# Four convolution layers on one core: another order for the last image of layer 1, the first signs' shift on another engine, narrower gate weights

## The chip, the cores and the metric

The kernel runs on one core of a Trainium2 chip. TensorE (PE in the profile; PEld is its weight load) multiplies matrices, VectorE (DVE), ScalarE (ACT) and GpSimd (POOL) do the rest, and SyncE (SP) issues most transfers. Each engine works through its own queue in order and waits on semaphores for the others. The metric is the device time of one execution in microseconds (us); less is better.

## The reference

Sixteen images of 256 channels and 28 x 28 pixels go through four layers. Layer 0 is a 3x3 convolution of signs, normalized over the batch, added to its input. Layer 1 is the one that the change touches; layer 2 is two more 3x3 convolutions of signs with batch norms, and layer 3 is attention over the 784 pixels of each image. Layer 1, cut to what matters:

```python
residual = prelu(x, a_alpha1)
y = conv3x3(sign(x + a_move), clip(a_w, -1, 1))
y = prelu(bn(y, a_bn1), a_alpha2)
y = se_gate(s * x + y * (1 - s)) * y          # first gate
y = bn(y * residual, a_bn2) + residual
u = conv1x1(sign(y + f_move), clip(f_w, -1, 1))
u = prelu(bn(u, f_bn1), f_alpha2)
u = se_gate(s2 * y + (1 - s2) * u) * u        # second gate
return bn(u, f_bn2) + y

def se_gate(mix):                             # per image
    h = relu(mix.mean(pixels) @ w1.T + b1)    # 256 -> 32
    return sigmoid(h @ w2.T + b2)             # 32 -> 256
```

Layer 2 begins with a batch norm over all images of layer 1's result, so it can't start before the last image's second gate is known.

## The kernel before

The 256 channels are two halves of 128 partitions (`k` for inputs, `mo` for outputs), and an image is a tile of 128 x 2 x 784. Layers run one after the other. In layers 0 to 2 each engine's order is the order in which the program's lines are called, under a manual schedule: no scheduler moves anything on TensorE, VectorE or ScalarE. `keep_busy(n)` puts n multiplications of a tile of zeros into TensorE's queue, whose result nobody reads.

**Layer 1's start.** `norm` (line 187) works out layer 0's scale `r` (`rsqrt`, line 137: a square root on ScalarE, the rest on VectorE) and two shifts, one for the sign (`zb1`) and one for the values (`bi0`). The shifts are made by three `nc.gpsimd.tensor_tensor` (lines 209 and 211). Its argument `then` issues `enter(0, 0)` on VectorE as soon as `r` is there; `sign1(0, 0)` on ScalarE needs both this and `zb1`. `transform` (line 696) then adds and subtracts neighbouring rows of the signs into `vs16`, `widen` copies that to `vs`, and TensorE convolves.

**The 3x3 convolution** (`conv`, line 724) makes two rows of output from four transformed inputs u = 0 to 3: for one `mo` and one `u`, 12 multiplications (6 of a high part of the weights with `vs16`, 6 of a low part with `vs`). `conv_pair` (743) collects u = 1 and 2 in the halves `i` = 0 and 1 of one PSUM tile, u = 0 and 3 in those of another; there are three such tiles of two banks (`psc`, line 427). `sum_pair_a` (754, ScalarE) and `sum_pair_b` (761, VectorE) turn the first pair into `uv`; `rows_out` (769, VectorE) adds each half of the second to it: one instruction for the even rows, one for the odd. `prelu_y` (789) finishes `y` and its sum.

**The gates.** Both gates of an iteration are asked together, since they are small: the first of image b-1, and the second of image b-2. `hidden_x` and `hidden_a` (792, 796) mix their sums into a tile `p` on VectorE, with one column for each gate, and multiply it with `w_1` (`hidden_sums`, 636), a tile of 128 columns in which 0 to 31 hold the first gate's weights, 32 to 63 the second's, and the rest zeros. `hidden_b` (802) makes the two relus on ScalarE; `gates` (809) multiplies with `w_2`, takes the sigmoid and a scale. `branch1_a`, `_b` and `_c` (822 to 835) apply the first gate and make the signs `z2` for `conv1x1` (839); `unit_u` and `unit_b` (854, 861) finish its result `u`; `branch2` (864) applies the second gate and sends the image to memory (`x2d`, GpSimd's queue, line 873). `squares2` (881) adds up squares for the next batch norm.

**The loop.** `iteration(b)` (888) interleaves three images: b in the convolution, b-1 at its first gate and conv1x1, b-2 at its second gate; `ahead` stands for the next image's entry, which the last iteration doesn't have. After the last (line 1017 on) comes a chain with one image left: both gates (image 15's first, image 14's second), image 15's branch 1 and conv1x1, `branch2` and `squares2` of image 14, then image 15's second gate, the moments of the batch norm (`moments1`) and the first signs of layer 2 (line 1110). `squares` and `products` write their full-size results, which nobody reads, into two buffers `rn` that they share.

Of the kernel before, what the change touches and what calls it, by code (L numbers as in the profile page):

```python
# [39 lines left out]
P = 128  # L40
# [43 lines left out]
def forward(ctx: ExitStack, tc: tile.TileContext, d: dict, out: bass.AP, careful: bool):  # L84
# [51 lines left out]

    def rsqrt(name, v, half=None):

        r, t = (const.tile(list(v.shape), F32, name=name + q) for q in ("_r", "_t"))
        A.activation(t, v, AF.Sqrt)  # L140
        V.reciprocal(r, t)
        tt(t, r, r, ALU.mult)
        if half is not None:
            tt(r, r, half, ALU.mult)
        else:
            V.tensor_scalar(r, r, -0.5, None, ALU.mult)
        tt(t, t, v, ALU.mult)
        V.scalar_tensor_tensor(r, t, -3.0, r, ALU.add, ALU.mult)
        return r
# [37 lines left out]
    def norm(name, moments, gamma, beta, sf=None, then=lambda r: None, shifts=()):  # L187


        half, e = vtile(name + "_half"), vtile(name + "_e")  # L190
        V.tensor_scalar(half, gamma, -0.5, None, ALU.mult)
        if sf is not None:

            tt(e, sf, sf, ALU.mult)
            V.tensor_scalar(e, e, 1e-30, 1.0 / EPS, ALU.max, ALU.mult)
            V.reciprocal(e, e)
        m, var = moments()
        v, c = vtile(name + "_v"), vtile(name + "_c")
        if sf is not None:
            tt(v, var, e, ALU.add)  # L200
        else:
            V.tensor_scalar(v, var, EPS, None, ALU.add)
        r = rsqrt(name, v, half)
        then(r)
        if not shifts:
            tt(c, m, r, ALU.mult)
            return r, tt(c, beta, c, ALU.subtract)
        cs = [vtile(f"{name}_c{i}") for i in range(len(shifts))]
        nc.gpsimd.tensor_tensor(c, m, r, ALU.mult)
        for o, b in zip(cs, shifts):  # L210
            nc.gpsimd.tensor_tensor(o, b, c, ALU.subtract)
        return r, *cs
# [214 lines left out]
    with tc.tile_pool(name="ps_conv", bufs=3, space=PSUM) as psc, \  # L427
# [13 lines left out]
        with tc.tile_pool(name="ph1", bufs=1) as ph:  # L441
# [106 lines left out]

            w_1, w_2, b_1 = (ph.tile(sh, F32, name=n) for sh, n in (([P, 2, P], "se1"), ([P, 256], "se2"), ([64, 1], "seb")))

# [84 lines left out]

            def hidden_sums(p):

                ps = pss.tile([P, 2], F32, tag="sm", name="hid")
                for k in range(2):
                    T.matmul(ps, lhsT=w_1[:, k, :], rhs=p[:, :, k], start=(k == 0), stop=(k == 1))  # L640
                return [ps[32 * g:32 * g + 32, g:g + 1] for g in range(2)]
# [100 lines left out]

            def conv_pair(b, mo, i, u):
                if i == 0:
                    pairs[b, mo, u > 0 and u < 3] = conv_ps()
                conv(b, mo, u, pairs[b, mo, u > 0 and u < 3][:, i, :HN])

# [20 lines left out]

            def rows_out(b, mo):
                ps, uv = pairs.pop((b, mo, False)), pairs.pop((b, mo))  # L770
                y = full("yu", f"y{b}_{mo}", 6)
                ys[b, mo] = y
                two = y.rearrange("p (a two b) -> p two a b", two=2, b=S)
                for i in range(2):
                    V.scalar_tensor_tensor(
# [15 lines left out]

            def hidden_x(t):
                p = small.tile([P, 2, 2], F32, tag="g0", name="g0")
                return tt(p, sums_of(t)[0], mix_x, ALU.mult)

            def hidden_a(t, p):

                r = small.tile([P, 2, 2], F32, tag="g1", name="g1")
                tt(r, sums_of(t)[1], mix_y, ALU.mult)
                return hidden_sums(tt(p, p, r, ALU.add))  # L800

            def hidden_b(t, sums):
                h = hidden[t % 3]
                for g, ps in enumerate(sums):
                    rows = slice(32 * g, 32 * g + 32)
                    A.activation(h[rows, g:g + 1], ps, AF.Relu, bias=b_1[rows])
                return h

            def gates(h, f=None):

                ps = pss.tile([P, 2, 2], F32, tag="sm", name="gate")
                g = small.tile([P, 2, 2], F32, tag="gate", name="gates")
                for k in range(2):
                    T.matmul(ps[:, k], lhsT=w_2[:, k * P:(k + 1) * P], rhs=h, start=True, stop=True)
                A.activation(g.rearrange("p i k -> p k i"), ps, AF.Sigmoid)
                if f is not None:
                    return tt(f, g[:, 1], s_bn[:, 3], ALU.mult)
                return tt(g, g, s_bn[:, 1::2], ALU.mult)

# [68 lines left out]
            def iteration(b):  # L888


                ahead, one, two = b + 1 < B, b >= 1, b >= 2
                if b + 2 < B:
# [9 lines left out]
                if two:  # L902
                    unit_u(b - 2, 1)
                if ahead:
                    enter(b + 1, 0, sc0)
                if one:
                    prelu_y(b - 1, 1)
                if ahead:
                    enter(b + 1, 1, sc0)
                    sign1(b + 1, 0)  # L910
                if two:
# [4 lines left out]
                h = hidden_a(b, hidden_x(b)) if one else None  # L916
                if ahead:
                    residual_a(b + 1, 0)
                    sign1(b + 1, 1)
                sum_pair_b(b, 0)  # L920
                if one:
                    h = hidden_b(b, h)
                if ahead:
                    residual_a(b + 1, 1)
                    residual_b(b + 1, 0)
                    transform(b + 1, 1)
                    residual_b(b + 1, 1)
                conv_pair(b, 0, 1, 3)
# [3 lines left out]
                else:  # L932
                    gate_bias()
                if ahead:
                    transform(b + 1, 2)
                if one:
                    for k in range(2):
                        branch1_a(b - 1, k, g[:, 0])
                if ahead:
                    widen(b + 1, 1)  # L940
                for i, u in enumerate((1, 2)):
# [10 lines left out]
                if one:  # L952
                    branch1_c(b - 1, 1)
                if ahead:
                    widen(b + 1, 2)
                if two:
# [6 lines left out]
                for s in aside[b + 1]:  # L963
                    s.load()
                if ahead:
                    for u in (0, 3):
                        transform(b + 1, u)
                        widen(b + 1, u)
                    for i, u in enumerate((0, 3)):
                        conv_pair(b, 1, i, u)  # L970
                    rows_out(b, 1)
                    for late in lates:
                        late()
                    if one:
                        conv1x1(b - 1)
                else:
                    conv1x1(b - 1)
                    for k in range(2):
                        unit_u(b - 1, k)
                        unit_b(b - 1, k)  # L980
                    for i, u in enumerate((0, 3)):
                        conv_pair(b, 1, i, u)
                    px = hidden_x(B)
                    rows_out(b, 1)
                    prelu_y(b, 1)
                    return px

# [5 lines left out]
            with tc.manual_schedule(engines={ET.PE, ET.DVE, ET.Activation}):  # L993
# [17 lines left out]
                for k in range(2):  # L1011
                    residual_b(0, k)
                for b in range(B):
                    px = iteration(b)


                b = B - 1
                keep_busy(14)
                g = gates(hidden_b(B, hidden_a(B, px)))
                keep_busy(14)  # L1020
# [14 lines left out]
                squares(x2[b][:, 0, :], shift[:, 0:1], sum_vv[:, 0:1])  # L1035
                for k in range(2):
# [5 lines left out]
                px = hidden_x(B + 1)  # L1042
                V.tensor_reduce(m1, sum_x2[:, :, 0:B - 1], AX.X, ALU.add)
# [737 lines left out]
```

## Time and profile before

| | us |
|---|---|
| median of 3 runs (lowest, highest) | 964.71 (964.29, 966.12) |
| profiled execution: its time | 964.49 |
| profiled execution: span, first to last instruction | 962.7 |
| busy in the span: TensorE | 942.6 (98%) |
| VectorE | 772.7 (80%) |
| ScalarE | 718.7 (75%) |
| GpSimd | 143.0 (15%) |
| layer 1: first to last convolution matmul | 115.6 to 448.9 |
| first matmul of layer 2 | 469.5 |

The span leaves out 1.8 us of the execution's time. A busy TensorE is not TensorE at its peak, and where `keep_busy` runs it is not even useful. In the rows below, "[2.97 <-POOL l_c]" means that the engine was idle for so long before the instruction, and what ended that. A group such as "x4" is a run of instructions of one line, given by its first start and the time to its last end. The granted clock is TensorE's, as a share of full speed.

### The profile page before, as it was taken

To read this page: it belongs to the slowest core of one execution; us is meant where nothing else is said; L and a number is where in the kernel's file an instruction comes from. 1 tells how busy PE (TensorE), PEld (TensorE's weight loads), DVE (VectorE), ACT (ScalarE), POOL (GpSimd) and SP (SyncE) were. 2 spreads that over 40 slices of the span, in tenths; PEclk is the share of its full clock that TensorE was granted. 3 is DMA by queue.
4 is the path that set the end of the run, shared out by engine and by line. 5 is a ranking of instruction groups with operands and counts; after the bars stand their busy time and mean duration, and the time that the engine had idled before them with its cause. 6 is when DMAs were issued, how large, how long until landed. Compare 5 with 4: busy or idle time off the path is not lost.

```text
span 962.7 us, 14797 instructions
## 1 busy us (share of the span) xinstructions
PE 942.6 (98%) x5615; PEld 582.4 (60%) x5615; DVE 772.7 (80%) x1416; ACT 718.7 (75%) x1198; POOL 143.0 (15%) x152
## 2 busy tenths in 40 slices
PE   8999999999999999999999999999999999999996
PEld 4555577788788788786555555555444444444442
DVE  4777798999988898976799988999656868677765
ACT  6887668888887888865888868888666666676652
POOL 3001100000000000000100000000145353434331
PEclk9999999999999999999999999999999999999998
DMA  9978512444433243000670000000143443435212
GB/s 352 343 267 292 192 34 84 139 143 153 146 104 101 101 134 117 34 35 34 253 316 1 1 1 2 1 1 1 16 79 75 90 113 81 121 73 130 67 67 105
DMA packets 26948, 105.82 MB, mean 110 GB/s; under 512 B 3490, under 2 KB 7268, under 8 KB 26868
## 3 DMA queue, kind: packets, MB, share of 16 engines
q1 hardware_dynamic: 20948, 73.44, 21.3%
q0 software_dynamic: 5632, 30.54, 11.6%
q8 instruction: 46, 0.75, 0.3%
q10 hardware_dynamic: 288, 0.80, 0.2%
q14 instruction: 34, 0.28, 0.1%
HBM read 72.67 MB, written 32.11 MB: 109 GB/s over the span
## 4 chain that ended last, share of the span: by engine, by line
PE 41%; DVE 7%; ACT 2%; issue 1%; DVEq 0%; ACTq 0%
PE cv L346 14%; PE sc L1356 8%; PE av L1377 8%; PE mi L1333 4%; DVE p L1144 2%; PE sm L1419 2%; PE mi L1437 2%; PE sm L1377 1%; DVE ab L360 1%; DVE l2c_fin L1146 1%; DVE l2b_fin L1146 1%; ACT fpads L1110 1%; ACT es L1360 0%; DVE r L1403 0%; DVE p L1320 0%
## 5 line engine op out<-in xcount | busy, mean ns | idle before, releaser
L346 PE MATMUL cv<-fpads,wpk 128*128 128x392 f16 (+1 forms) x1746 | 294.8, 331 | 2.4 <-DVE wpk L273 1.2
L730 PE MATMUL cv<-vs,w 128*128 128x392 bf16 (+1 forms) x1536 | 285.3, 354 | 2.3 <-DVE vs L134 2.3
L346 PEld LDWEIGHTS <-wpk 128*128 128x128 f16 x1746 | 169.1, 97 | 128.9 <-DVE wpk L273 2.9
L730 PEld LDWEIGHTS cv<-vs,w 128*128 128x128 f32 x768 | 142.1, 190 | 10.9
L1360 ACT ACTIVATE es<-sc 128x784 f32<-128x784 f32 x112 | 87.3, 822 | 41.4 <-PE sc L1356 41.4
L730 PEld LDWEIGHTS <-w 128*128 128x128 f16 x768 | 67.6, 101 | 57.0 <-issue 17.2
L1356 PE MATMUL sc<-q,keyswa 64*128 64x392 f32 x448 | 89.9, 513 | 0.9 <-ACT es L1360 0.9
L357 ACT ACTIVATE t<-cv,rounding 128x392 f32<-128x392 f32 (+2 forms) x82 | 52.0, 634 | 41.2 <-PE cv L346 41.2
L1144 DVE SCALAR_TENSOR_TENSOR p<-ab,vec 128x392 f32<-128x392 f32 x128 | 79.1, 618 | 2.3
L1377 PE MATMUL av<-es,v 128*64 128x392 f32 x448 | 80.7, 499 | 0.0
L1370 POOL TENSOR_TENSOR sum<-sum,es 128x784 f32<-128x784 f32 x32 | 67.2, 2099 | 3.1 <-ACT es L1360 0.6
L1356 PEld LDWEIGHTS sc<-q,keyswa 64*128 64x128 f32 x448 | 38.9, 186 | 44.0 <-issue 17.1
L873 POOL DMA_DIRECT2D x2d<-x x16 | 8.6, 537 | 339.7 <-DVE x L867 281.0
L1344 DVE COPY keyswa<-mi 64x392 f32<-64x392 f32 x31 | 16.3, 564 | 52.7 <-ACT q L1340 52.7
L1377 PEld LDWEIGHTS av<-es,v 128*64 128x64 f32 x448 | 29.4, 136 | 47.4 <-issue 47.0
L712 ACT CAST vs<-vs 128x840 fp32r<-128x840 bf16 x63 | 54.1, 882 | 2.9 <-DVE vs L134 2.9
L845 PE MATMUL cv<-z,fw 128*128 128x392 f32 x256 | 48.9, 342 | 1.0 <-ACT z L837 0.8
L360 DVE SCALAR_TENSOR_TENSOR ab<-ab,cv 128x392 f32<-128x392 f32 x64 | 35.4, 553 | 16.3 <-ACT ab L358 16.3
L845 PEld LDWEIGHTS cv<-z,fw 128*128 128x128 f32 x256 | 45.7, 188 | 2.3 <-ACT z L837 2.1
L1333 PE MATMUL mi<-p,wqk 128*128 128x392 f32 x124 | 45.1, 505 | 0.1
L439 PE MATMUL unused<-idle 128*128 128x512 bf16 x175 | 41.2, 393 | 3.0 <-POOL idle L475 3.0
L1368 POOL TENSOR_TENSOR sum<-es 128x784 f32<-128x784 f32 x16 | 30.0, 1877 | 91.0 <-ACT es L1360 91.0
(289 smaller groups left out, 1516.9 us busy)
## 6 DMA issues: line engine op xcount, KB each, us to landing
xs<-in_x_dram SPq DMA_DIRECT2D x30, 784.0 KB, 6.1
x2d<-x POOLq DMA_DIRECT2D x16, 784.0 KB, 3.6
out_dram<-p SPq DMA_DIRECT2D x15, 784.0 KB, 3.8
p<-x2d POOLq DMA_DIRECT2D x14, 784.0 KB, 6.8
p<-x2d SPq DMA_DIRECT2D x13, 784.0 KB, 15.4
n0d<-n POOLq DMA_DIRECT2D x16, 392.0 KB, 5.9
n<-n0d SPq DMA_DIRECT2D x16, 392.0 KB, 3.2
st<-in_w_dram SPq DMA_DIRECT2D x12, 384.0 KB, 6.4
```

Of the source, the lines that this page charges most:

```text
L346: T.matmul(pss[j][:, n // size if careful else h, :rows * S].rearrange("p (a b) -> p a b", b=S), lhsT=w[:, n, t, :], rhs=pads[:, blocks[j] ...
L357: A.activation(by_halves(t, blocks[j]), ps, AF.Identity, bias=rounding, scale=1.0 / PACK)
L360: V.scalar_tensor_tensor(a, b, -PACK, ps, ALU.mult, ALU.add)
L712: copy(v, w)
L730: T.matmul(ps.rearrange("p (a b) -> p a b", b=S), lhsT=w[:, k, c, u, mo * P:(mo + 1) * P], rhs=v[:, b % 2, u, k, :, c:c + S], start=((part ...
L845: T.matmul(ps[:, h, :HN], lhsT=w[:, k, mo * P:(mo + 1) * P], rhs=z2[b][:, k, h * HN:(h + 1) * HN], start=(k + i == 0), stop=(k + i == 2),)
L1144: V.scalar_tensor_tensor(p, y, alpha[:, mo:mo + 1], y, ALU.mult, ALU.max)
L1333: T.matmul(ps[:, h, :HN], lhsT=wqk[:, k, :], rhs=x[b][:, k, h * HN:(h + 1) * HN], start=(k == 0), stop=(k == 1))
L1356: T.matmul(ps[:, h, :HN], lhsT=chunk[rows], rhs=qs[b][rows], start=True, stop=True)
L1360: A.activation(e, ps[:, :, :HN], AF.Exp, scale=0.125)
L1370: (V if late else nc.gpsimd).tensor_tensor(sums[b, late], sums[b, late], e, ALU.add)
L1377: T.matmul(ps[64 * h:64 * h + 64, :HN], lhsT=w, rhs=e[:, h, :], start=start, stop=stop)
```

## The change

It has three parts.

1. **The last iteration gets a function of its own** (`last_iteration`), and `iteration` loses its `ahead` cases. In it the gates of the last regular kind come before the convolution of u = 0 instead of after it; conv1x1 of image 14 comes between the convolutions of u = 1 and 2 of the second half of the outputs; and image 14's second gate is asked alone, ahead of image 15's first. For that, `conv_pair` and `rows_out` can do their work in pieces, and the gates' functions take a slice (`ONE`, `TWO`) of their two columns. After the loop, only image 15's first gate is left to ask, `branch2` of image 14 is done, half of its squares are done on ScalarE and the other half becomes a product on VectorE, and the last gate asks for one column alone.
2. **The shifts of layer 0's norm** are made by four ScalarE activations of one column (two per shift) from `r` and the negated mean; that mean is negated on VectorE while it waits for the root.
3. **`w_1` has 64 columns** instead of 128, and so has the PSUM tile `hid` 64 partitions.

```diff
-    def rsqrt(name, v, half=None):
+    def rsqrt(name, v, half=None, beside=None):
...
         A.activation(t, v, AF.Sqrt)
+        if beside:
+            beside()
...
-        r = rsqrt(name, v, half)
+        r = rsqrt(name, v, half, (lambda: V.tensor_scalar(less, m, -1.0, None, ALU.mult)) if shifts else None)
...
-        nc.gpsimd.tensor_tensor(c, m, r, ALU.mult)
         for o, b in zip(cs, shifts):
-            nc.gpsimd.tensor_tensor(o, b, c, ALU.subtract)
+            for k in range(2):
+                A.activation(o[:, k:k + 1], r[:, k:k + 1], AF.Identity, bias=b[:, k:k + 1], scale=less[:, k:k + 1])
...
-            w_1, w_2, b_1 = (ph.tile(sh, F32, name=n) for sh, n in (([P, 2, P], "se1"), ([P, 256], "se2"), ([64, 1], "seb")))
+            w_1, w_2, b_1 = (ph.tile(sh, F32, name=n) for sh, n in (([P, 2, 64], "se1"), ([P, 256], "se2"), ([64, 1], "seb")))
...
-            def hidden_sums(p):
+            def hidden_sums(p, some=slice(0, 2)):
...
-                ps = pss.tile([P, 2], F32, tag="sm", name="hid")
+                ps = pss.tile([64, 2], F32, tag="sm", name="hid")
                 for k in range(2):
-                    T.matmul(ps, lhsT=w_1[:, k, :], rhs=p[:, :, k], start=(k == 0), stop=(k == 1))
+                    T.matmul(ps[:, some], lhsT=w_1[:, k, :], rhs=p[:, some, k], start=(k == 0), stop=(k == 1))
...
-            def conv_pair(b, mo, i, u):
-                if i == 0:
+            def conv_pair(b, mo, i, u, parts=range(2)):
+                if i == 0 and 0 in parts:
                     pairs[b, mo, u > 0 and u < 3] = conv_ps()
-                conv(b, mo, u, pairs[b, mo, u > 0 and u < 3][:, i, :HN])
+                conv(b, mo, u, pairs[b, mo, u > 0 and u < 3][:, i, :HN], parts)
...
-            def rows_out(b, mo):
+            def rows_out(b, mo, rows=range(2)):
...
-            def hidden_b(t, sums):
+            def hidden_b(t, sums, some=BOTH):
                 h = hidden[t % 3]
-                for g, ps in enumerate(sums):
+                for g, ps in list(enumerate(sums))[some]:
...
+            def last_iteration(b):
+
+                conv_pair(b, 0, 0, 1)
+                conv_pair(b, 0, 1, 2)
+                for k in range(2):
+                    unit_u(b - 2, k)
+                prelu_y(b - 1, 1)
+                for k in range(2):
+                    unit_b(b - 2, k)
+                sum_pair_a(b, 0)
+                h = hidden_b(b, hidden_a(b, hidden_x(b)))
+                conv_pair(b, 0, 0, 0)
+                sum_pair_b(b, 0)
+                g = gates(h)
+                for k in range(2):
+                    branch1_a(b - 1, k, g[:, 0])
+                conv_pair(b, 0, 1, 3)
+                branch2(b - 2, 0, g[:, 1])
+                for k in range(2):
+                    branch1_b(b - 1, k)
+                    branch1_c(b - 1, k)
+                conv_pair(b, 1, 0, 1)
+                rows_out(b, 0)
+                squares2(b - 2, 0)
+                branch2(b - 2, 1, g[:, 1])
+                conv1x1(b - 1)
+                sum_pair_a(b, 1)
+                prelu_y(b, 0)
+                conv_pair(b, 1, 1, 2)
+                for k in range(2):
+                    unit_u(b - 1, k)
+                    unit_b(b - 1, k)
+                squares2(b - 2, 1)
+                px = hidden_x(B, TWO)
+                conv_pair(b, 1, 0, 0, (0,))
+                h = hidden_a(B, px, TWO)
+                sum_pair_b(b, 1)
+                h = hidden_b(B, h, TWO)
+                conv_pair(b, 1, 0, 0, (1,))
+                rows_out(b, 1, (0,))
+                g = gates(h, some=TWO)
+                conv_pair(b, 1, 1, 3)
+                branch2(b - 1, 0, g[:, 1])
+                squares2(b - 1, 0)
+                px = hidden_x(B, ONE)
+                rows_out(b, 1, (1,))
+                prelu_y(b, 1)
+                keep_busy(10)
+                h = hidden_a(B, px, ONE)
+                branch2(b - 1, 1, g[:, 1])
+                return h
...
-                keep_busy(14)
-                g = gates(hidden_b(B, hidden_a(B, px)))
+                h = last_iteration(b)
+                g = gates(hidden_b(B, h, ONE), some=ONE)
...
-                for k in range(2):
-                    branch2(b - 1, k, g[:, 1])
-
-                products(x2[b][:, 1, :], shift[:, 1:2], x2[b][:, 1, :], sum_vv[:, 1:2])
+                for i, v in ((b, sum_vv[:, 1:2]), (b - 1, sum_sq[:, 1, b - 1:b])):
+                    products(x2[i][:, 1, :], shift[:, 1:2], x2[i][:, 1, :], v)
...
-                V.scalar_tensor_tensor(d1, shift, float(N), sv, ALU.mult, ALU.add)
+                tt(d1, sv, sum_x2[:, :, b - 1], ALU.add)
+                V.scalar_tensor_tensor(d1, shift, 2.0 * N, d1, ALU.mult, ALU.add)
...
-                h = hidden_a(B + 1, px)
                 for k in range(2):
-                    squares2(b - 1, k)
-                h = hidden_b(B + 1, h)
+                    squares(us[b, k], 0.0, sum_uu[:, k:k + 1], (B * N)**-0.5)
+                h = hidden_b(B + 1, hidden_a(B + 1, px, TWO), TWO)
...
-                squares(us[b, 0], 0.0, sum_uu[:, 0:1], (B * N)**-0.5)
...
-                g = gates(h, dqg[:, 2])
-                squares(us[b, 1], 0.0, sum_uu[:, 1:2], (B * N)**-0.5)
+                g = gates(h, dqg[:, 2], TWO)
```

More of the change, by code (lines that the diff above doesn't have):

```diff
@@ L197, in norm @@
         m, var = moments()
-        v, c = vtile(name + "_v"), vtile(name + "_c")
+        v, c, less = vtile(name + "_v"), vtile(name + "_c"), vtile(name + "_less") if shifts else None
         if sf is not None:
@@ L767, in sum_pair_b @@
                 pairs[b, mo] = uv
-            def rows_out(b, mo):
[L770 to L774, printed above, removed]
+            def rows_out(b, mo, rows=range(2)):
+                ps, uv = pairs[b, mo, False], pairs[b, mo]
+                if 0 in rows:
+                    ys[b, mo] = full("yu", f"y{b}_{mo}", 6)
+                two = ys[b, mo].rearrange("p (a two b) -> p two a b", two=2, b=S)
+                for i in rows:
                     V.scalar_tensor_tensor(
@@ L790, in prelu_y, with hidden_x, hidden_a @@
                 prelu(ys[b, mo], "a_alpha2", ra2, mo, sums_of(b + 1)[1][:, 0, mo:mo + 1])
-            def hidden_x(t):
+            BOTH, ONE, TWO = slice(0, 2), slice(0, 1), slice(1, 2)
+            def hidden_x(t, some=BOTH):
                 p = small.tile([P, 2, 2], F32, tag="g0", name="g0")
-                return tt(p, sums_of(t)[0], mix_x, ALU.mult)
-            def hidden_a(t, p):
+                tt(p[:, some], sums_of(t)[0][:, some], mix_x[:, some], ALU.mult)
+                return p
+            def hidden_a(t, p, some=BOTH):
                 r = small.tile([P, 2, 2], F32, tag="g1", name="g1")
-                tt(r, sums_of(t)[1], mix_y, ALU.mult)
-                return hidden_sums(tt(p, p, r, ALU.add))
-            def hidden_b(t, sums):
+                tt(r[:, some], sums_of(t)[1][:, some], mix_y[:, some], ALU.mult)
+                tt(p[:, some], p[:, some], r[:, some], ALU.add)
+                return hidden_sums(p, some)
+            def hidden_b(t, sums, some=BOTH):
                 h = hidden[t % 3]
-                for g, ps in enumerate(sums):
+                for g, ps in list(enumerate(sums))[some]:
                     rows = slice(32 * g, 32 * g + 32)
@@ L807, in hidden_b, with gates @@
                 return h
-            def gates(h, f=None):
+            def gates(h, f=None, some=BOTH):
                 ps = pss.tile([P, 2, 2], F32, tag="sm", name="gate")
@@ L813, in gates @@
                 for k in range(2):
-                    T.matmul(ps[:, k], lhsT=w_2[:, k * P:(k + 1) * P], rhs=h, start=True, stop=True)
-                A.activation(g.rearrange("p i k -> p k i"), ps, AF.Sigmoid)
+                    T.matmul(ps[:, k, some], lhsT=w_2[:, k * P:(k + 1) * P], rhs=h[:, some], start=True, stop=True)
+                A.activation(g.rearrange("p i k -> p k i")[:, :, some], ps[:, :, some], AF.Sigmoid)
                 if f is not None:
                     return tt(f, g[:, 1], s_bn[:, 3], ALU.mult)
-                return tt(g, g, s_bn[:, 1::2], ALU.mult)
+                tt(g[:, some], g[:, some], s_bn[:, 1::2][:, some], ALU.mult)
+                return g
             z2 = [None] * B
@@ L888, in iteration @@
             def iteration(b):
-                ahead, one, two = b + 1 < B, b >= 1, b >= 2
+                one, two = b >= 1, b >= 2
                 if b + 2 < B:
@@ L903, in iteration @@
                     unit_u(b - 2, 1)
-                if ahead:
-                    enter(b + 1, 0, sc0)
+                enter(b + 1, 0, sc0)
                 if one:
                     prelu_y(b - 1, 1)
-                if ahead:
-                    enter(b + 1, 1, sc0)
-                    sign1(b + 1, 0)
+                enter(b + 1, 1, sc0)
+                sign1(b + 1, 0)
                 if two:
@@ L916, in iteration @@
                 h = hidden_a(b, hidden_x(b)) if one else None
-                if ahead:
-                    residual_a(b + 1, 0)
-                    sign1(b + 1, 1)
+                residual_a(b + 1, 0)
+                sign1(b + 1, 1)
                 sum_pair_b(b, 0)
@@ L922, in iteration @@
                     h = hidden_b(b, h)
[L923 to L927, printed above, removed]
+                residual_a(b + 1, 1)
+                residual_b(b + 1, 0)
+                transform(b + 1, 1)
+                residual_b(b + 1, 1)
                 conv_pair(b, 0, 1, 3)
@@ L933, in iteration @@
                     gate_bias()
-                if ahead:
-                    transform(b + 1, 2)
+                transform(b + 1, 2)
                 if one:
@@ L938, in iteration @@
                         branch1_a(b - 1, k, g[:, 0])
-                if ahead:
-                    widen(b + 1, 1)
+                widen(b + 1, 1)
                 for i, u in enumerate((1, 2)):
@@ L953, in iteration @@
                     branch1_c(b - 1, 1)
-                if ahead:
-                    widen(b + 1, 2)
+                widen(b + 1, 2)
                 if two:
@@ L964, in iteration @@
                     s.load()
[L965 to L976, printed above, removed]
-                    conv1x1(b - 1)
-                    for k in range(2):
[L979 to L986, printed above, removed]
+                for u in (0, 3):
+                    transform(b + 1, u)
+                    widen(b + 1, u)
@@ new lines, in iteration @@
+                for i, u in enumerate((0, 3)):
+                    conv_pair(b, 1, i, u)
+                rows_out(b, 1)
+                for late in lates:
+                    late()
+                if one:
+                    conv1x1(b - 1)
+            def last_iteration(b):
[48 more added lines that the diff above has]
+                return h
@@ L1012, in forward @@
                     residual_b(0, k)
-                for b in range(B):
-                    px = iteration(b)
+                for b in range(B - 1):
+                    iteration(b)
                 b = B - 1
-                keep_busy(14)
-                g = gates(hidden_b(B, hidden_a(B, px)))
+                h = last_iteration(b)
+                g = gates(hidden_b(B, h, ONE), some=ONE)
                 keep_busy(14)
@@ L1035, in forward @@
                 squares(x2[b][:, 0, :], shift[:, 0:1], sum_vv[:, 0:1])
-                for k in range(2):
-                    branch2(b - 1, k, g[:, 1])
-                products(x2[b][:, 1, :], shift[:, 1:2], x2[b][:, 1, :], sum_vv[:, 1:2])
+                for i, v in ((b, sum_vv[:, 1:2]), (b - 1, sum_sq[:, 1, b - 1:b])):
+                    products(x2[i][:, 1, :], shift[:, 1:2], x2[i][:, 1, :], v)
                 last = wpool.tile([P, 2, N], F32, tag="wa", name="last")
-                px = hidden_x(B + 1)
+                px = hidden_x(B + 1, TWO)
                 V.tensor_reduce(m1, sum_x2[:, :, 0:B - 1], AX.X, ALU.add)
```

## Prediction

> **What bounds the kernel now.** I read four views, from coarse to fine. The chain of waits came first and says little of layer 1: it breaks off at 467.65 us, where layer 2 begins, so what bounds layer 1 must be read from stretches. The table of stretches (engines with their busy us, then granted clock, DMA share, GB/s):
>
> ```profile
> 115.00:116.00 1.00, 0.38 (x3) 0.24 (x4) 0.67 (x2) 0.99 (x2) 0.00 (x0) 1.00 0.78 135
> 200.00:300.00 100.00, 100.00 (x576) 80.70 (x575) 91.05 (x192) 86.79 (x133) 2.66 (x5) 1.00 0.38 125
> 426.00:449.00 23.00, 22.15 (x127) 17.44 (x126) 13.57 (x31) 11.79 (x18) 0.53 (x1) 1.00 0.13 53
> 449.00:460.00 11.00, 10.24 (x53) 6.22 (x50) 8.53 (x22) 5.57 (x9) 0.53 (x1) 1.00 0.00 0
> ```
>
> In the 16 iterations of layer 1 (115.6 to 449 us) TensorE is never idle, VectorE has 9% to spare and ScalarE 13%. So every instruction taken from TensorE there is worth its own length, and every start of TensorE that is put forward too. Before (112 to 115.6) and after (449 to 469.5) stands a chain through all engines: there TensorE's "busy" is mostly filler (`keep_busy`), and a step counts by its latency. Layers 2 and 3 are untouched and only move.
>
> **1. Shift of the first signs.** The timeline of the start:
>
> ```profile
> 112.12 1.03 DVE L686 SCALAR_TENSOR_TENSOR xs<-n,l_r,xs 128x784 f32<-128x784 int16 x1
> 112.17 1.04 POOL L209 TENSOR_TENSOR l_c<-l_mv,l_r 128x2 f32<-128x2 f32 x1 [0.64 <-DVE l_r L148]
> ...
> 113.29 0.88 POOL L211 TENSOR_TENSOR l_c<-moved,l_c 128x2 f32<-128x2 f32 x1
> ...
> 114.20 1.79 ACT L692 ACTIVATE pad<-xs,l_c 128x784 bf16<-128x784 f32 x2 [2.97 <-POOL l_c L211]
> 115.18 0.67 DVE L134 TENSOR_TENSOR vs<-pad 128x420 bf16<-128x420 bf16 x2 [1.06 <-ACT pad L692]
> ```
>
> The scale is there at 112.09; GpSimd needs until 114.17 for two 128x2 operations, and the sign waits for that, though its data (the first `enter`) are ready at 113.16, after the read of the accumulator. Now four 128x1 ACTIVATEs do it (two per shift), ahead of the sign in ScalarE's queue. The trace has no 128x1 ACTIVATE with both pointers; nearest is `hidden` (32x1, one pointer): 0.52 us for two, 0.26 each. Four: 112.15 + 4 x 0.26 = 113.2, level with the data. [...] By the row it is 114.20 - 113.2 = 1.0. I take 0.95, near the row; ends 0.5 and 1.05. The added VectorE operation (minus the mean) lies in the 0.27 us for which VectorE waits for the root. TensorE starts as much sooner; next in line is VectorE's `transform`, which moves along.
>
> **2. First gate weights of 64 columns.** Weight loads grouped by shape (mean ns after the comma), and TensorE in one iteration:
>
> ```profile
> L1377 PEld LDWEIGHTS av<-es,v 128*64 128x64 f32 x448 | 29.4, 136 | 47.4 <-issue 47.0
> L640 PEld LDWEIGHTS hid<-g,se 128*128 128x128 f32 x68 | 10.0, 191 | 0.7 <-DVE g L134 0.4 <-issue 0.2
> ```
>
> ```profile
> 280.28 6.68 PE L730 MATMUL cv<-vs,w 128*128 128x392 bf16 x36
> 286.80 0.50 PE L640 MATMUL hid<-g,se 128*128 128x2 f32 x4
> 287.17 2.32 PE L730 MATMUL cv<-vs,w 128*128 128x392 bf16 x12
> ```
>
> One convolution matmul takes (286.80 - 280.28)/36 = 0.181 us. The four of `hid` hold TensorE 0.37 us though they stream two columns: they wait for their weights. The shapes say what 64 columns cost: 136 against 191 ns, 55 less. The first of four loads hides under the last convolution matmul, three are bare: 3 x 55 = 0.16 us per gate. Fifteen gates lie in the untouched iterations (the one for the bias, and those of iterations 1 to 14): **2.4 us**. Ends: 0, and 15 x 4 x 55 ns = 3.3. [...]
>
> **3. The last iteration** (426.78 to 448.86, 22.08 us). Old: 96 convolution matmuls at 0.181 (17.4), 16 of conv1x1 (2.85, by their pitch of 0.178), `hid` and `gate` at 0.36 each, and 0.85 us of wait for the second sign of `z`; 21.8 of the 22.1. New: that wait goes, since the gate is asked one convolution sooner and conv1x1 comes one convolution later: branch1_a at about 434.5, z at 437.6 and 438.5, conv1x1 at 438.2 with its second channel half at 438.9. `hid` is 0.2 instead of 0.36; the lone second gate adds 0.2 + 0.36. And one **new wait**: the last convolution writes the other half of the PSUM tile whose first half `rows_out` reads, and in TensorE's program that matmul now waits for VectorE. From the start of the matmul before: 0.36 to its end, 0.62 for the VectorE row, some 0.08 of hand-over, 1.06 us, of which 0.54 is covered by that matmul and the gate: 0.5 lost, with the whole rest of TensorE's queue behind it. Sum 17.4 + 2.85 + 0.2 + 0.36 + 0.56 + 0.5 = 21.9: the iteration ends about where it did, **0.0** (ends 0.3 gained, 1.0 lost). ScalarE and VectorE have the room: 11.8 and 13.6 of 23 us busy, and what is added (a multiply-add and a square of image 14) fits under the last convolution. The store of image 14 leaves some 6 us sooner, on a GpSimd queue that had been idle for 13.79 us.
>
> **4. After the last convolution, to the gate.**
>
> ```profile
> 449.05 1.16 DVE L775 SCALAR_TENSOR_TENSOR y<-cv,us,uvs 128x392 f32<-128x392 f32 x2 [0.68 <-PE cv L730]
> ...
> 452.43 0.52 ACT L806 ACTIVATE hidden<-hid,seb 32x1 f32<-32x1 f32 x2 [5.27 <-PE hid L640]
> ...
> 465.12 0.17 ACT L815 ACTIVATE gates<-gate 128x4 f32<-128x4 f32 x1
> ...
> 466.15 1.28 ACT L1071 ACT_TABLE_LOAD   x1
> ```
>
> One of two rows is done before: 0.54. One of two `hidden` activations goes: 0.26. Four bare loads (TensorE waits here): 0.21. Together **1.0** (ends 0.7 and 1.1). The filler of ten (216 ns each, 2.2 us) ends just as the sums arrive.
>
> **5. From conv1x1 of image 15 to layer 2.** VectorE sheds two multiply-adds of image 14 and gets one product. It does not profit: that product takes the `rn` buffer in which ScalarE squares until 458.65, so it starts at 458.7, not 457.6; with three tiny operations instead of two the last `unit_b` starts at 461.7, not 461.35: 0.35 lost. Then 64 columns (0.21) and one `hidden` less (0.26), but the square of the last half, now ahead of `hidden` on ScalarE, ends at 463.85 and eats some of that: the gate's matmul is about where it was, 464.15. The gain lies behind it: the squares of `u` are over, so the sigmoid comes at 464.8, the table load runs at 465.0, not 466.15, and the variance no longer waits for the last square (466.17) but for VectorE: 465.9. The root comes at 466.9 instead of 467.56, and the filler before layer 2 keeps TensorE until 468.9, so layer 2 starts 0.55 sooner: **0.55** (ends 0 and 1.3).
>
> **Sum.** 0.95 + 2.4 + 0.0 + 1.0 + 0.55 = 4.9 us, from the profiled execution's span of 962.7 to 957.8; with 1.8 around it 959.6, against its own time of 964.49. That execution lies 0.2 under the median, so I say **959.8**.
>
> **Rivals.**
> (a) *The column cut saves nothing* because the loads' spacing is set elsewhere. For it: no 64-column load of this trace stands between two-column matmuls. Against: 191 and 136 ns differ by what the columns make. Without 2.4 and some 0.4 in the tail: 962.6.
> (b) *The new order waits more than once*: the second `hid` asks for sums that are ready only some 0.15 us ahead of it. Each late step blocks all of TensorE's queue; 1 to 2 us more: 961.3.
> (c) *The loop's other engines take back half of the 2.4.* VectorE at 91% speaks for it, no single TensorE wait between 117 and 440 us against: 961.0.
> (d) *Slower: the clock.* The tail has four fillers fewer ahead of the gate and a wait more. The stretch 950 to 954 us, with TensorE busy 1.82 of 4 us, is followed by 8 us at a granted clock of 0.50. If that struck at 449 us, the fillers (10, 14 and 14 at 0.22) would double and delay the gate, `z` and `hid` by 2.2, 2.6 and 3, and conv1x1 by 2.9: 10.7 less 4.9, about 970.5. It decides once the halved clock lasts over some 5 us of matmuls. Against it: no wait here is above 1 us, and the 2.1 us pause at 113.5 left the clock at 1.00.
>
> **Chances.** Forecast 0.62, (a) 0.10, (b) 0.14, (c) 0.11, (d) 0.03. A measurement tells 0.2% (1.9 us) from no change, so the bound is 962.8. The forecast, (b), (c) and half of (a) are faster, half of (a) is no change, (d) is slower: 0.92, 0.05, 0.03. The terms' ends add up to 957.7 and 964.5 or so; the range 957.9 to 962.4 takes in (b), (c) and most of (a).
>
> **What will show it.** The sign at about 113.2; four `hid` matmuls of 0.20 us and a period of 20.77 where it was 20.93; TensorE waiting about 0.5 us for `rows_out` in the last iteration; one `hidden` in each tail gate; the table load right behind the sigmoid. A `hid` of 0.37 would refute the largest term.

## The result, and the profile after

The changed kernel takes 963.13 us (median of 22 runs, 962.49 to 964.22) beside 965.19 for the kernel before (22 runs, 963.1 to 966.12): a ratio of 0.9982, 95% interval 0.9976 to 0.9989, so 1.7 us faster (1.1 to 2.3), where 4.9 were forecast. The profiled execution took 963.05 us, its span 961.3.

Layer 1 is best compared between two events in it, the start of the operation that makes the scale (`l_r`) and the first convolution matmul of layer 2; neither layer 0 nor layer 3 plays a part then. That stretch is 357.55 us before and 356.41 after: 1.14 us less. By parts, from the starts in both traces (us):

| | before | after | forecast of the difference | measured |
|---|---|---|---|---|
| scale to first convolution | 3.69 | 2.83 | -0.95 | -0.86 |
| first convolution to last iteration | 311.16 | 311.87 | **-2.4** | **+0.71** |
| last iteration, to its last convolution matmul | 21.88 | 22.22 | 0.0 | +0.34 |
| on to image 15's conv1x1 | 8.14 | 7.12 | -1.0 | -1.02 |
| on to layer 2 | 12.68 | 12.36 | -0.55 | -0.32 |

The first row, in the timeline of the changed kernel's start:

```profile
112.31 0.66 ACT L213 ACTIVATE l_c<-l_r,moved,l_less 128x1 f32<-128x1 f32 x2 [0.89 <-DVE l_r L150]
112.31 1.03 DVE L688 SCALAR_TENSOR_TENSOR xs<-n,l_r,xs 128x784 f32<-128x784 int16 x1
...
112.88 0.65 ACT L213 ACTIVATE l_c<-l_r,vec,l_less 128x1 f32<-128x1 f32 x2
...
113.53 1.83 ACT L694 ACTIVATE pad<-xs,l_c 128x784 bf16<-128x784 f32 x2
```

The shift is done while VectorE makes the data, and the sign follows at once: 1.22 us from the start of the activations, where GpSimd took 2.03.

The second row is the surprise. Weight loads by shape, then TensorE in one iteration and its load queue there, of the changed kernel:

```profile
L642 PEld LDWEIGHTS hid<-g,se 128*64 128x64 f32 x72 | 5.5, 136 | 5.5 <-DVE uvs L768 3.9 <-issue 1.3 <-DVE g L134 0.3
```

```profile
279.92 6.68 PE L732 MATMUL cv<-vs,w 128*128 128x392 bf16 x36
286.53 0.39 PE L642 MATMUL hid<-g,se 128*64 128x2 f32 x4
286.86 2.33 PE L732 MATMUL cv<-vs,w 128*128 128x392 bf16 x12
```

```profile
285.69 0.56 PEld L732 LDWEIGHTS cv<-vs,w 128*128 128x128 f32 x3
286.53 0.31 PEld L642 LDWEIGHTS hid<-g,se 128*64 128x64 f32 x4 [0.28 <-DVE uvs L768]
286.85 0.28 PEld L732 LDWEIGHTS <-w 128*128 128x128 f16 x3
```

And the load queue of the kernel before at the same place:

```profile
285.86 0.76 PEld L730 LDWEIGHTS cv<-vs,w 128*128 128x128 f32 x4
286.61 0.61 PEld L640 LDWEIGHTS hid<-g,se 128*128 128x128 f32 x4
287.06 0.21 PEld L730 LDWEIGHTS <-w 128*128 128x128 f16 x2
```

A load now takes 136 ns, exactly as forecast, and the loads follow each other in half the time (55 to 59 ns apart, where the bare ones were 109 to 112 apart). But ahead of the first there is a gap of 0.28 us that wasn't there. Before, the first load began 3 ns after the last convolution matmul did, under it; with 64 columns it begins 278 ns after that matmul's start. (The releaser named, `uvs` on VectorE, is not the cause: from iteration 2 on the load's own operand, `g`, has been ready for 0.86 us or more, and the gap is the same in all iterations.) `hid`'s last matmul and the next convolution are parted by 130 ns instead of 111, too. So `hid` holds TensorE for 0.33 us (from 286.53 to 286.86), where 0.37 were there before and 0.20 were forecast, and an iteration takes 20.98 us, where 20.93 were there before and 20.77 were forecast.

The rest, in the timeline of the last iteration and the tail:

```profile
447.06 2.34 PE L732 MATMUL cv<-vs,w 128*128 128x392 bf16 x12 [0.38 <-DVE y L777]
...
449.43 0.63 DVE L777 SCALAR_TENSOR_TENSOR y<-cv,us,uvs 128x392 f32<-128x392 f32 x1 [1.20 <-PE cv L732]
...
452.07 0.25 ACT L812 ACTIVATE hidden<-hid,seb 32x1 f32<-32x1 f32 x1 [2.78 <-PE hid L642]
...
458.04 1.03 DVE L886 SCALAR_TENSOR_TENSOR product<-x,shift 128x784 f32<-128x784 f32 x1 [0.87 <-ACT square L883]
...
464.02 0.17 ACT L821 ACTIVATE gates<-gate 128x2 f32<-128x2 f32 x1 [0.70 <-PE gate L820]
464.21 1.28 ACT L1105 ACT_TABLE_LOAD   x1
```

Here stand the wait for `rows_out` (0.38 us, forecast 0.5), one row and one `hidden` where there were two, the product held by the shared buffer, and the table load right behind the sigmoid.

### The profile page after: what moved, and what is told of

Its sections match the earlier page's. It is cut to its first block, busy times and chain, and to the rows that moved or that the text cites. A ratio compares the mean times of both kernels' runs of the same rounds, so it can differ in the third digit from the quotient of the medians.

```text
span 961.3 us, 14808 instructions
## 1 busy us (share of the span) xinstructions
PE 942.2 (98%) x5613; PEld 578.4 (60%) x5619; DVE 773.4 (80%) x1424; ACT 719.0 (75%) x1200; POOL 140.9 (15%) x149
## 4 chain that ended last, share of the span: by engine, by line
PE 84%; DVE 9%; ACT 3%; issue 1%; DMA 1%; SPq 1%; DVEq 0%; ACTq 0%
PE cv L732 29%; PE cv L348 22%; PE sc L1390 8%; PE av L1411 8%; PE cv L852 4%; PE mi L1367 4%; DVE p L1178 2%; PE sm L1453 2%; PE mi L1471 2%; PE sm L1411 1%; DVE ab L362 1%; DMA xs<-in_x_dram 1%; DVE l2c_fin L1180 1%; DVE l2b_fin L1180 1%; PE hid L642 1%
```

## The experiments

Theory W: a load of 64 columns can't be pulled ahead of the 128-column matmul before it, and so the narrow gate costs more than it saves where TensorE is busy. Rival F: the narrowing brings what the forecast says, and the shift or the order took it away. All times are medians; "under" is by the ratio to the kernel before, run beside.

**128 columns again.** In the changed kernel:

```diff
-... ([P, 2, 64], "se1") ...
+... ([P, 2, 128], "se1") ...
...
-ps = pss.tile([64, 2], F32, tag="sm", name="hid")
+ps = pss.tile([128, 2], F32, tag="sm", name="hid")
```

> The changed kernel, but the gates' first weights and their PSUM tile have 128 columns again. Theory W (a 64-column load can't be pulled ahead of the 128-column convolution before it, so the narrow gate costs TensorE 0.05 us more in the loop and saves 0.26 us in each tail gate): 17 gates x 0.05 = 0.9 us won back, 2 x 0.26 = 0.5 us lost, so 0.4 us faster than the changed kernel, some 2.3 us under the kernel before; hid takes 0.36 us and the convolution matmul before it 0.19 us again. Rival F (the forecast: narrow loads save 0.16 us each, and something else took it away): about 2.8 us slower than the changed kernel, slower than the kernel before.

Measured: 962.65 us, ratio 0.9978 (0.9971 to 0.9986): 2.1 us under the kernel before and about 0.4 under the changed one. That is W's number (the two intervals overlap), and F's, 2.8 us slower, is far outside. The trace has the convolution matmul before `hid` at 0.19 us again, 311.23 us for the loop (0.64 won back), and 0.22 us more on the way to conv1x1.

**The columns alone**, the same two lines of the diff in the other direction, in the kernel before.

> The kernel before with 64 columns in the gates' first weights and nothing else. Theory W: 16 gates x 0.05 = 0.8 us lost in the loop, 0.5 us gained in the two tail gates, so 0.3 us slower than before; 280 ns from the last convolution matmul to the first of hid. Rival F: 2.9 us faster.

Measured: 966.40 us, 1.0021 (1.0012 to 1.0029): slower, as W says and F doesn't. In the trace the loop takes 311.90 us instead of 311.16, W's 0.8. The 0.5 us that W gave to the two tail gates did not come: to conv1x1 it is 8.11 us instead of 8.14, and on to layer 2 12.65 instead of 12.68. There the filler runs right up to `hid`, and behind it, too, the load of 64 columns starts late: it begins 0.31 us after the start of the last filler matmul, where the one of 128 columns began 0.06 and 0.13 us after it. Without the start of layer 1, which by chance was 0.61 us shorter in this execution (3.08; see the last experiment), the stretch is 0.75 us longer than before. The ratio's 2.0 us is still more; the runs spread from 964.73 to 968.25 and the profiled one, with 964.73, is their lowest, so the trace does not show where the others lose the rest. The ten above 966 us have a mean granted clock of 0.993 to 0.995, the other four 0.995 or 0.996. What causes the rest stays open.

**The shift alone**, the first part of the change in the kernel before.

> The kernel before with the shifts of the first signs on ScalarE and nothing else. Both theories: the first convolution matmul of layer 1 starts 0.85 us sooner after the scale is there, and all of it arrives at the end: 0.7 to 1.0 us faster. Rival: the earlier start is lost on a later wait in the loop, then the time is as before and TensorE waits somewhere between 117 and 440 us.

Measured: 964.06 us, 0.9991 (0.9983 to 1.0): 0.9 us. The start takes 2.83 us instead of 3.69, and in the loop TensorE waits nowhere: 311.25 us. The interval touches no change, but the stretch of layer 1 is 0.69 us shorter in the trace.

**The order alone**: the changed kernel with 128 columns and the shifts on GpSimd.

> The kernel before with the last iteration's order and the tail's changes only: 128 columns, and the shifts on GpSimd as before. If the three parts add up, this is the 128-column kernel's gain (0.22%) less that of the shift alone (0.09%): about 1.2 us faster than before, made of 1.0 us between the last convolution and the first tail gate, 0.3 to 0.5 us behind it, and nothing or 0.3 us lost in the last iteration, where one TensorE wait of 0.4 us for rows_out stands. Rival: the new order alone is worth nothing, and the parts don't add.

Measured: 963.51 us, 0.9988 (0.9982 to 0.9995): 1.2 us, the expected number. In the trace it is made of -0.80 us on the way to conv1x1, -0.41 from there to layer 2 and +0.17 in the last iteration. The parts add up: -0.9 (shift), -1.2 (order) and +0.4 (columns, in the changed kernel) make -1.7, though each of them is known to some 0.7 us only.

**96 columns**, as the first experiment with 96 for 128.

> The changed kernel with 96 columns in the gates' first weights. Theory W1 (the load can be pulled ahead as long as the width rounds up to the whole array of 128): 190 ns before hid as with 128 columns, and three bare loads of about 84 ns instead of 111: 0.08 us less per gate than with 128 columns, 1.3 us in all under the kernel with 128 columns. Theory W2 (any width but that of the matmul before it has to wait): 280 ns before hid, about 0.03 us more per gate than with 128 columns, the time between those of 64 and 128 columns. Rival F: half of the narrowing's gain.

Measured: 962.60 us, 0.9972 (0.9963 to 0.9981): by the ratio 0.6 us, by the medians nothing under 128 columns, where W1 gave 1.3. In the trace W1 holds: 188 ns before `hid`, then 283 to the next convolution matmul where 128 columns take 364. TensorE in one iteration:

```profile
264.78 0.72 PE L732 MATMUL cv<-vs,w 128*128 128x392 f32 x3
265.34 0.42 PE L642 MATMUL hid<-g,se 128*96 128x2 f32 x4
265.62 2.31 PE L732 MATMUL cv<-vs,w 128*128 128x392 bf16 x12
```

The loop takes 310.01 us, 1.22 less than with 128 columns. This execution's start was 0.56 us longer than those of the other kernels with the shift on ScalarE, since VectorE waited 0.59 us for the integers' transfer (`n`). What hides it in the medians is told in part below under the clock.

**66 columns**, so that the width is just over half of 128.

> The changed kernel with 66 columns in the gates' first weights. Theory W1 (any width over half of the array counts as the whole array, so the load is pulled ahead, and its length goes by the columns): 190 ns before hid, loads 59 ns apart, hid 0.21 us where 128 columns take 0.36: 16 x 0.15 = 2.4 us under the kernel with 128 columns in the loop and 0.4 us in the tail, some 5 us under the kernel before. Rival W3 (the load's length goes in steps of 32 columns): as with 96 columns, hid 0.28 us and 2.7 us under the kernel before. Rival W2 (it has to wait like 64 columns): as the changed kernel.

Measured: 959.62 us, 0.9945 (0.9931 to 0.9958), 5.3 us under the kernel before: W1's number. One iteration, and the loads by shape:

```profile
263.66 0.91 PE L732 MATMUL cv<-vs,w 128*128 128x392 f32 x4
264.41 0.35 PE L642 MATMUL hid<-g,se 128*66 128x2 f32 x4
264.62 2.31 PE L732 MATMUL cv<-vs,w 128*128 128x392 bf16 x12
```

```profile
L642 PEld LDWEIGHTS hid<-g,se 128*66 128x66 f32 x72 | 6.9, 139 | 2.3 <-issue 1.1 <-DVE g L134 0.5
```

`hid` takes 0.21 us: a load of 139 ns, hardly more than the 136 of 64 columns, and no gap. The four widths side by side, from the starts of one regular iteration (ns):

| columns | last convolution matmul to first of `hid` | first of `hid` to next convolution | sum | loop, us |
|---|---|---|---|---|
| 128 | 185 | 364 | 549 | 311.23 |
| 96 | 188 | 283 | 471 | 310.01 |
| 66 | 187 | 208 | 395 | 308.86 |
| 64 | 279 | 326 | 605 | 311.87 |

With 128 and with 96 columns every other iteration has 194 or 195 ns in the first column, for a sum of 558 or 478. From 128 to 66 each column saves about the same; at 64 there is a step of 210 ns.

**66 columns alone**, in the kernel before.

> The kernel before with 66 columns in the gates' first weights and nothing else: the forecast's second step alone, made with a width that the load can be pulled ahead with. Theory W1: hid 0.21 us for 0.36, 16 x 0.15 = 2.4 us in the loop and 0.4 us in the two tail gates: 2.8 us faster than before. Rival: in the kernel before some other engine sets the loop's period once TensorE has 0.15 us less, and less than 1.5 us arrives.

Measured: 962.70 us, 0.9975 (0.9965 to 0.9985): 2.4 us. The loop takes 308.84 us, 2.32 less, without a wait of TensorE in it: VectorE and ScalarE keep up. The last iteration brings 0.18 us and the two tail gates 0.34, 2.8 in all, as expected. So the forecast's 2.4 us were there to be had in the kernel before, with 66 columns instead of 64.

**A PSUM tile of its own** for the last convolution, in the 66-column kernel:

```diff
-            def rows_out(b, mo, rows=range(2)):
-                ps, uv = pairs[b, mo, False], pairs[b, mo]
+            def rows_out(b, mo, rows=range(2), ps=None):
+                ps, uv = ps or pairs[b, mo, False], pairs[b, mo]
...
-                conv_pair(b, 1, 1, 3)
+                own = conv_ps()
+                conv(b, 1, 3, own[:, 1, :HN])
...
-                rows_out(b, 1, (1,))
+                rows_out(b, 1, (1,), own)
```

> The 66-column kernel with a PSUM tile of its own for the last convolution of the last iteration, so that it need not wait until VectorE has read the other half of the tile. If that wait is on the path: TensorE's wait of 0.4 us for rows_out is gone and the time falls by 0.3 to 0.5 us. Rival: the last rows_out is then held by VectorE's other work and nothing is gained.

The last iteration of this kernel's trace, in which the second gate and the last convolution now follow each other without a wait:

```profile
442.95 0.50 PE L820 MATMUL gate<-hidden,se 128*128 128x1 f32 x4
443.31 2.31 PE L732 MATMUL cv<-vs,w 128*128 128x392 bf16 x12
```

Measured: 960.32 us, 0.9945 (0.9931 to 0.9959), no better than without it by the ratio. In the trace the last iteration takes 21.18 instead of 21.71 us and all of it reaches layer 2 (352.36 instead of 352.90). What hides it in the median is told below under the clock.

**Other buffers for two products**, in the kernel just above:

```diff
-def products(x, bias, y, out, op=ALU.add):
-    V.scalar_tensor_tensor(full("rn", "product", 2), ...)
+def products(x, bias, y, out, op=ALU.add, at=("rn", "product", 2)):
+    V.scalar_tensor_tensor(full(*at), ...)
...
-products(x2[i][:, 1, :], shift[:, 1:2], x2[i][:, 1, :], v)
+products(x2[i][:, 1, :], shift[:, 1:2], x2[i][:, 1, :], v, at=("yu", "product", 6))
```

> The kernel with its own PSUM tile, and the two products after image 15's first gate written to other buffers than those that ScalarE's squares use. If the shared buffer is what costs there: VectorE's wait of 0.87 us before the second product goes, the second unit_b starts 0.2 to 0.35 us sooner, and the time falls by as much. Rival: ScalarE's unit_u sets unit_b's start, and nothing is gained.

Measured: 958.78 us, 0.9943 (0.9929 to 0.9956). The wait of 0.87 us is gone, and conv1x1 to layer 2 takes 12.00 us instead of 12.36: the upper end of what was expected. The ratio alone would not show it.

**The last two once more, side by side on one chip.**

> The 66-column kernel once more, beside the next one. About 5.3 us under the kernel before.

> The 66-column kernel with its own PSUM tile and the other buffers for the two products, once more, beside the 66-column kernel on the same chip. If both waits were on the path, it is 0.5 + 0.35 = 0.85 us under that; if what happens later takes the gain away, the two are the same within 0.3 us.

Measured: 960.23 us, 0.9952 (0.994 to 0.9965), and 958.92 us, 0.9943 (0.9932 to 0.9955). The traces repeat to 0.02 us (352.88 and 351.99 us of layer 1, 0.89 apart), the medians are 1.3 us apart, and the ratios' intervals overlap. Of all versions run, this last has the lowest medians: 5.5 us under the kernel before, 3.8 more than the change brought.

**GpSimd first**, in the kernel before:

```diff
         r = rsqrt(name, v, half)
-        then(r)
         if not shifts:
+            then(r)
...
             nc.gpsimd.tensor_tensor(o, b, c, ALU.subtract)
+        late = vtile(name + "_late")
+        nc.gpsimd.tensor_copy(late, r)
+        then(late)
         return r, *cs
```

> The kernel before, with VectorE's first enter held back until GpSimd has made both shifts (it takes a copy of the scale that GpSimd writes after them). Theory S (GpSimd's small operations took 1.04 and 0.88 us because VectorE's multiply-add ran at the same time): each takes 0.2 us now, with VectorE idle. Rival: they take about 1 us each whenever they come first, and then do so here too. Slower than before in both cases, by 0.2 to 1 us more or less, since enter waits for four GpSimd operations.

The start of this kernel, GpSimd and VectorE alone:

```profile
112.73 0.20 POOL L209 TENSOR_TENSOR l_c<-l_mv,l_r 128x2 f32<-128x2 f32 x1 [0.64 <-DVE l_r L148]
112.87 0.18 POOL L213 COPY l_late<-l_r 128x2 f32<-128x2 f32 x1
113.01 0.19 POOL L211 TENSOR_TENSOR l_c<-moved,l_c 128x2 f32<-128x2 f32 x1
113.09 1.03 DVE L689 SCALAR_TENSOR_TENSOR xs<-n,l_late,xs 128x784 f32<-128x784 int16 x1 [0.45 <-POOL l_late L213]
113.16 1.02 POOL L211 TENSOR_TENSOR l_c<-vec,l_c 128x2 f32<-128x2 f32 x1
```

S holds here: 0.20, 0.18 and 0.19 us for those that start while VectorE is idle, and 1.02 for the one that starts during its multiply-add and ends 0.06 us after it. The copy ran ahead of the two subtractions (GpSimd's order is not under the manual schedule), so `enter` waited for two operations and not for four. With that, the expectation of a slower kernel failed: the first convolution is 3.15 us after the scale instead of 3.69, and the one run took 963.89 us.

## Why the prediction was wrong

**The step that failed** is the second: "The first of four loads hides under the last convolution matmul, three are bare: 3 x 55 = 0.16 us per gate." The 55 ns are right (the loads came 55 to 59 ns apart where the bare ones had been 109 to 112 apart, some 53 less). The first half of the sentence was taken from the trace of 128 columns and carried over to 64. The four widths show what stands in its place: a load of 66, 96 or 128 columns begins 2 to 4 ns after the start of the 128-column matmul before it; one of 64 begins only 278 ns after it, which puts `hid` off by 279 - 187 = 92 ns against 66 columns. Another 118 ns go behind `hid`'s first matmul: 52 ahead of the second and 70 ahead of the next convolution, less 4 of the loads. The fifteen gates of the loop add up to 0.62 us more than with 128 columns (605 ns each instead of 549 or 558; only in iteration 1, where the load waited for its operand before, 0.12 us less), and 0.71 were measured for the loop. Forecast and outcome of this term differ by 3.1 us, most of the 3.8 by which the stretch of layer 1 misses the forecast.

That it isn't narrow loads as such, the trace of the kernel before could have told, in layer 3, where loads of 128, 64 and 32 columns follow each other. TensorE and then its load queue:

```profile
692.84 2.90 PE L1333 MATMUL mi<-p,wqk 128*128 128x392 f32 x8
695.67 1.53 PE L1419 MATMUL sm<-p,wv 128*32 128x196 f32 x32
```

```profile
695.67 1.15 PEld L1419 LDWEIGHTS sm<-p,wv 128*32 128x32 f32 x32 [0.56 <-issue]
```

Where the columns change from 128 to 32, the load begins 0.42 us after the start of the matmul before it, in all 15 places; where they stay at 128, 64 or 32, it begins after 2 ns in the median. The changes between 128 and 64 columns, in both directions, take 0.42 us too (there the rows change as well). So the delay goes with the change of shape, once on the way in and once on the way out, and 66 columns behave as no change from 128. Why that is so, and why the step lies between 64 and 66, no run shows.

Rival (a) named the place ("no 64-column load of this trace stands between two-column matmuls") but only let the saving go to nothing, 962.6 us; that the measured 963.13 lies near it is chance, since the spacing of the loads, which it held fixed, did shrink, from 111 to 58 ns. The length of a load was never wrong: 136 ns were forecast and measured. What mattered was when the first one began.

**The others, point by point.**
- The shift: -0.86 for -0.95, right. The four activations took 1.22 us, where the row of `hidden` gives 4 x 0.26 = 1.04; that the forecast stayed a little under that row's gain of 1.0 was the author's estimate. But part of the gain is a matter of timing: with GpSimd the start took 3.69 and 3.70 us in two kernels and 3.08, 2.78 and (with `enter` behind GpSimd) 3.15 in three others, by which of its operations took 0.2 us and which 0.8 to 1.04. The 2.78 is even less than the 2.83 with ScalarE.
- The last iteration: +0.34 for 0.0. The new wait was there, 0.38 for 0.5. With 128 columns the order alone costs 0.17, with 66 next to nothing (21.71 us, 21.70 in the old order). The 0.51 from there to 22.22 belong to the 64 columns: two gates at about 0.21 each make most of it.
- To the gate: -1.02 for -1.0, right: the order alone brought 0.80 (forecast for one row and one activation: 0.54 + 0.26), the columns 0.22 (forecast: 0.21). In the new order TensorE is idle for 0.11 us ahead of `hid`, and there 64 columns save what they should; in the old order, right behind the filler, they saved 0.03.
- To layer 2: -0.32 for -0.55. The product waited for ScalarE's buffer (0.87 us), as foreseen, and the table load moved ahead. The term that was mis-sized is the root: it came 2.49 us after the sigmoid where 2.1 were forecast (466.9 - 464.8). VectorE's small operations paced it, and one of them took 0.58 us instead of 0.17:

```profile
464.56 1.82 POOL L114 MEMSET fpads<- 128x120 f16 x4 [11.25 <-DVE product L886]
464.88 0.58 DVE L1101 TENSOR_SCALAR l_v<-l_v 128x2 f32<-128x2 f32 x1
466.51 0.20 ACT L230 ACTIVATE l2a_t<-l_v 128x2 f32<-128x2 f32 x1 [0.79 <-DVE l_v L134]
```

  In the kernel before, GpSimd's fill of `fpads` (for layer 2) came behind that operation:

```profile
465.27 0.17 DVE L1066 TENSOR_SCALAR l_v<-l_v 128x2 f32<-128x2 f32 x1
466.19 1.82 POOL L114 MEMSET fpads<- 128x120 f16 x4 [6.74 <-ACT square L876]
```

  The fill moved ahead, since ScalarE's squares, for whose end it had waited, are over sooner, and the operation started within it. Without these 0.41 us the root would have come some 2.1 us after the sigmoid, an estimate (2.49 - 0.41); no run tried it.
- Rivals (b) to (d) did not come. TensorE waited in the new order once, at the place named; with 0.15 us less per iteration no other engine held it; and the clock at 449 us stayed at 1.00.

With 66 columns, all five terms stand beside the forecast as -0.86, -2.30, -0.17, -1.01 and -0.32: 4.7 us for 4.9, in a kernel that took 959.62 us where 959.8 were forecast for the change. The sum was right for another width; that it agrees so closely is in part luck, since -0.17 and -0.32 miss 0.0 and -0.55 in opposite directions.

## What to carry to other kernels

A short matmul between long ones is worth its weight loads, and here these went by columns (191 ns for 128, 164 for 96, 139 for 66, 136 for 64); but before a stationary tile is narrowed, ask whether its load still overlaps the matmul before it: here it does at 66 columns (it begins 2 to 4 ns after that matmul's start) and not at 64 (278 ns), so padding to 66 was worth 3.5 us over stopping at 64. A row that proves a duration doesn't prove that the overlap around it survives; look in the trace for places where loads of the two shapes follow each other, and read the gap there. And look at what VectorE does beside a small step on GpSimd: here one of 0.18 to 0.20 us took up to 1.04 beside VectorE's multiply-add of 1.03.

## What the runs showed of the hardware

**The end of the kernel falls on either side of a change of clock.** In the fourteen traces TensorE's clock is full from 5.8 to 8.5 us into the span on, for 942.1, 945.5, 948.9 or 952.3 us: the lengths are steps of 3.41 us apart. Then it halves to 0.50, in some traces ahead of the last 14 matmuls or amid them, in others after them. The stretches of the kernel before and of the changed kernel, granted clock ahead of the last two columns:

```profile
954.00:958.00 4.00, 2.09 (x14) 1.56 (x10) 2.14 (x5) 0.00 (x0) 0.00 (x0) 0.50 0.30 113
```

```profile
953.00:957.00 4.00, 1.07 (x14) 0.77 (x10) 2.14 (x5) 0.00 (x0) 0.00 (x0) 1.00 0.42 153
```

The same 14 matmuls keep TensorE busy for 2.09 or 1.07 us. From layer 2's first matmul to the last one of the kernel it is 486.08 us in the kernel before (halved ahead of them) and 485.22 in the changed one (not yet); to the end of the span, with what follows the last matmul, it is 493.23 and 492.75. So 0.48 us of the two profiled spans' difference (1.4) lie behind layer 1, where the change does nothing. The one with its own PSUM tile had 486.44 and 494.03, against 485.26 and 492.58 of the 66-column kernel beside it, which is why it looked no better than that.

The runs of one kernel fall apart by their mean granted clock, too. With its own PSUM tile, two took 958.37 and 958.95 us at 0.999, three 960.32 to 961.05 at 0.996 or 0.997. Of those at 0.998 or more, the three with 96 columns took 960.60 to 961.08 us and the seven with 128 columns 962.20 to 962.76: there the 1.3 us expected of 96 columns can be seen. Among the runs with a lower clock (eight and nine) the medians are 962.68 and 962.75; what takes the gain away in those is not shown.

**GpSimd's small operations took 0.80 to 1.04 us beside VectorE's multiply-add.** At the start of layer 1, seven operations on 128x2 elements that started while VectorE ran none took 0.18 to 0.20 us. Of nine that started during one, eight took 0.80 to 1.04 us and ended some 0.05 us after it; one (66 columns alone) took 0.20, so it isn't without exception.

**A small operation of VectorE took 0.58 us beside GpSimd's fill.** In all nine traces with the new tail, the `TENSOR_SCALAR` shown above started 0.06 or 0.07 us into the second of the four fills of `fpads` (0.63 us) and ended 0.02 us after it, in 0.58 us. In the five others, where the fill comes later, it took 0.17. No run moved the fill alone.
